# A second pair of sequences with two-level Strassen in the up-projections of a gated-scan and Hadamard-FFN kernel

## The chip, the cores and the metric

The kernel runs on one core of a Trainium2 chip, in float32 throughout. The metric is the device time of one execution in microseconds. The engines go by the names of the profile: PE (TensorE matmul), PEld (its weight loads), DVE (VectorE), ACT (ScalarE), POOL (GpSimd), SP (SyncE, which here only issues DMA transfers). Before the change the median of three runs is 791.53 us (791.39 to 792.0).

## The reference

```python
def attn(x, Wi, Wf, Wg, Wo, gnorm_w):            # x: (4, 512, 512)
    i, f, g = x @ Wi.T, x @ Wf.T, x @ Wg.T
    gate = sigmoid(f)
    v = silu(i) * (1 - gate)
    o = scan over t of  o[t] = gate[t] * o[t-1] + v[t]
    o = o * rsqrt(mean(o * o) + EPS) * gnorm_w * g * sigmoid(g)
    return o @ Wo.T

def ffn(x, W1, W2, W3):                          # hidden width 2048
    hidden = silu(x @ W1.T) * (x @ W3.T)
    return fwht(hidden) @ W2.T                   # Walsh-Hadamard along the 2048

x = x + layernorm(attn(layernorm(x), ...))
x = x + layernorm(ffn(layernorm(x), ...))
```

The batch is four sequences of 512 positions, each 512 wide. The transform is applied to W2 once instead of to the hidden values.

## The kernel before

**Strassen products.** Every large matrix product is cut into 2 x 2 blocks and made by seven block products in place of eight (the Winograd form; `ORDER` lists them, P1, P2, P6, P5, P7, P3, P4). The sums of blocks that this needs are made on DVE by `combine_left` (lines 156 to 163) and `combine_right` (165 to 173), each four adds or subtractions. The seven products of one unit go into three PSUM banks X, Y and Z; X is read out after P1, P6, P7 and P4, since each of them goes on from the sum before. A read-out (an "eviction") is a copy on ACT or an add on DVE (lines 492 and 494).

**Units.** An attention unit (`attn_unit`, three per sequence) and a single FFN unit (`ffn_unit`, for 2 x 128 of w1's and w3's columns, called a row block m; eight per sequence) are one such set of seven with 4 matmuls of 128 x 128 x 256 for each product, 28 in all (line 517). The products of the attention's output (`attn_out`, line 624) and of the FFN's output (`ffn_out`, line 684; four parts per sequence, 28 matmuls each) come piece by piece from the queue `fill` and stand between the products of a unit: one behind products 1, 3, 5 and 6, or behind all seven in a unit that is called dense.

**The pair.** For sequences 2 and 3 the FFN's up-projections are made together. The two sequences are the two column halves of one larger product, and a second Strassen level is laid over the first: `ffn_pair(g, down)` goes through seven outer steps (`OUTER`) of seven inner products ("leaves"), each 2 matmuls (line 879), 98 for two row blocks of both sequences. Each of the 49 leaves is evicted alone (ACT at line 889 for the plain products of outer P1 and P7, else DVE at line 892); some outer sums are added on POOL (894, 896). The weights of an outer step are loaded by `load_leaf_w` (four transfers of 128 KB, line 822) three steps ahead, and POOL makes their inner sums. `hidden` makes SiLU and the product (852, 860), and POOL combines half of the results. The down-projections of the group before (`down`, one matmul per piece) are spread between leaves 4 and 48.

The right-hand side of the pair, `xq`, lies in three double tiles and one single: B11 and B12 in `blocks[0]`, B21 and B22 in `blocks[1]`, T2 and T1 in `blocks[2]`, T4 alone. `transpose_pair` fills the first two from the folded copies of the normalized x; `combine_pair_early` makes T4 and T3 (four DVE operations of 128 x 1024), `combine_pair_late` makes T2 and T1 and the remaining inner sums, right before the pair.

**Folds.** A normalized x is written to DRAM by POOL (`xnd`, line 317), read back in 32-row blocks by SP (`load_fold`, eight transfers of 128 KB, line 437) and turned by 32 x 32 transposes on DVE (455, 770).

**The order.** After the attentions of sequences 0 to 2: FFN of sequence 0 (eight units), attention of sequence 3, FFN of sequence 1 (eight units), then the pair in four groups, then the last 56 down matmuls. In sequence 0's units w1 and w3 are read from the inputs, combined on DVE and kept in DRAM (`kept`, a POOL transfer); sequence 1 and the pair read them back. The steps for w2's transform (`low_pair`, `low_tile`, for four pairs of row blocks) stand beside units of sequence 0.

**Who sets the order.** PE's and SP's instructions run in the order of the code. For DVE, ACT and POOL a planner sets the order when the program is built, from estimated costs and from priorities (`high_priority`; evictions 400, steps beside them 200; `behind` and `issue_after` give an earliest place). At run time each engine's queue runs strictly in that order. Buffers are shared by tag: `w` (stream, 5), `w` (stream2, 4), `x` (3), `wide` (3), `xt` (2), `og` (1), `ht` (4); a tile waits until a buffer of its tag is free. `run` and `seven` hang the small steps (`acts`, `sums`, `scaled`, `beside`) behind products.

## Time and profile before

| | us |
|---|---|
| median of three runs | 791.53 |
| the profiled execution | 792.25 |
| its span, from the first to the last instruction | 790.5 |
| first instruction of the pair's products (line 879) | 490.0 |
| end of the last matmul | 780.45 |

The profile's parts used here: the busy time of each engine and its number of instructions; the span in 40 slices with the busy share in tenths; the chain of work that ended last, followed back from the end; groups of instructions by line with their mean duration; and, from the trace, the same by stretch (busy time of PE, its weight loads, DVE, ACT and POOL with the number of instructions, the granted clock, the DMA share and GB/s), the instructions in order of time, and the DMA transfers with the time from issue to landing. The granted clock is 0.996 over the span.

### The profile page before, as it was taken

To read this page: it belongs to the slowest core of one execution; us is meant where nothing else is said; L and a number is where in the kernel's file an instruction comes from. 1 tells how busy PE (TensorE), PEld (TensorE's weight loads), DVE (VectorE), ACT (ScalarE), POOL (GpSimd) and SP (SyncE) were. 2 spreads that over 40 slices of the span, in tenths; PEclk is the share of its full clock that TensorE was granted. 3 is DMA by queue.
4 is the path that set the end of the run, shared out by engine and by line. 5 is a ranking of instruction groups with operands and counts; after the bars stand their busy time and mean duration, and the time that the engine had idled before them with its cause. 6 is when DMAs were issued, how large, how long until landed. Compare 5 with 4: busy or idle time off the path is not lost.

```text
span 790.5 us, 10222 instructions
## 1 busy us (share of the span) xinstructions
PE 776.3 (98%) x3608; PEld 670.1 (85%) x3608; DVE 564.2 (71%) x1093; ACT 246.9 (31%) x348; POOL 245.5 (31%) x319
## 2 busy tenths in 40 slices
PE   9999999999999999999999999999999999999994
PEld 7888788888888888888888888888788888888884
DVE  6789889799789774477455459868755655765676
ACT  4374754543436212344223412011321200111112
POOL 2111202112213110001001005088947646672452
PEclk9999999999999999999999999999999999999998
DMA  9997445776997982538246736341521412141012
GB/s 296 398 340 299 156 198 180 218 258 244 339 336 289 340 325 102 160 150 347 94 187 200 267 78 221 131 122 33 195 80 54 157 53 58 49 166 54 1 53 108
DMA packets 78148, 144.93 MB, mean 183 GB/s; under 512 B 6160, under 2 KB 55952, under 8 KB 77712
## 3 DMA queue, kind: packets, MB, share of 16 engines
q1 hardware_dynamic: 68032, 96.82, 38.1%
q0 software_dynamic: 9344, 46.14, 14.9%
q10 hardware_dynamic: 720, 1.31, 0.4%
q8 instruction: 29, 0.48, 0.2%
q14 instruction: 23, 0.19, 0.1%
HBM read 97.06 MB, written 47.19 MB: 182 GB/s over the span
## 4 chain that ended last, share of the span: by engine, by line
PE 88%; DVE 5%; DMA 2%; POOL 1%; issue 1%; SPq 0%; ACT 0%; POOLq 0%; DVEq 0%
PE X_f L517 13%; PE X_po L684 13%; PE X_u L879 11%; PE X_a L517 10%; PE Z_po L684 7%; PE Z_f L517 6%; PE Z_u L879 5%; PE Z_a L517 5%; PE X_y L624 3%; PE Y_f L517 3%; PE Y_po L684 3%; PE Y_a L517 3%; PE Y_u L879 3%; PE Z_y L624 2%; DMA w2p<-in_W_dram 1%
## 5 line engine op out<-in xcount | busy, mean ns | idle before, releaser
L684 PE MATMUL X_po<-w,ht 128*128 128x256 f32 x512 | 132.1, 379 | 0.1
L517 PE MATMUL X_f<-xt_f,w 128*128 128x256 f32 x512 | 121.2, 380 | 0.1
L879 PE MATMUL X_u<-xq,wl 128*128 128x256 f32 x448 | 114.4, 381 | 2.3 <-ACT q L889 0.8
L517 PEld LDWEIGHTS X_f<-xt_f,w 128*128 128x128 f32 x512 | 96.8, 190 | 14.5 <-DVE d_f L492 0.5
L684 PEld LDWEIGHTS X_po<-w,ht 128*128 128x128 f32 x512 | 97.2, 190 | 13.7 <-DVE f L492 0.5
L879 PEld LDWEIGHTS X_u<-xq,wl 128*128 128x128 f32 x448 | 84.2, 190 | 17.1 <-issue 3.6
L892 DVE TENSOR_TENSOR q<-X_u,q 128x512 f32<-128x512 f32 x88 | 60.8, 691 | 42.6 <-PE X_u L879 41.7
L494 ACT COPY d_f<-X_f 128x512 f32<-128x512 f32 x48 | 28.0, 584 | 131.8 <-PE X_f L517 115.7
L684 PE MATMUL Z_po<-w,ht 128*128 128x256 f32 x256 | 66.4, 379 | 0.0
L492 DVE TENSOR_TENSOR f<-X_po,f 128x512 f32<-128x512 f32 x51 | 34.9, 685 | 36.9 <-PE X_po L684 36.9
L517 PE MATMUL Z_f<-xt_f,w 128*128 128x256 f32 x256 | 60.5, 379 | 0.0
L879 PE MATMUL Z_u<-xq,wl 128*128 128x256 f32 x224 | 57.6, 379 | 0.0
L684 PEld LDWEIGHTS Z_po<-w,ht 128*128 128x128 f32 x256 | 48.6, 190 | 6.8 <-DVE f L492 0.2
L517 PEld LDWEIGHTS Z_f<-xt_f,w 128*128 128x128 f32 x256 | 48.6, 190 | 6.6
L263 POOL TENSOR_TENSOR rs_f<-rs_f,power 128x2 f32<-128x2 f32 x16 | 13.4, 840 | 117.8 <-DVE nm_f L364 73.5
L852 ACT ACTIVATE q<-q 128x1024 f32<-128x1024 f32 x16 | 16.9, 1057 | 103.8 <-DVE q L892 58.2
L879 PEld LDWEIGHTS Z_u<-xq,wl 128*128 128x128 f32 x224 | 42.5, 190 | 6.0 <-DVE q L892 0.3
L892 DVE TENSOR_TENSOR q<-Z_u,q 128x512 f32<-128x512 f32 x48 | 33.1, 689 | 20.1 <-PE Z_u L879 19.5
L158 POOL TENSOR_TENSOR wl<-wl 128x256 f32<-128x256 f32 x28 | 21.3, 762 | 77.4 <-DMA wl<-s_w 70.2
L494 ACT COPY d_a<-X_a 128x512 f32<-128x512 f32 x36 | 21.1, 585 | 67.8 <-PE X_a L517 67.6
L889 ACT COPY q<-X_u 128x512 f32<-128x512 f32 x24 | 14.0, 584 | 89.4 <-PE X_u L879 76.8
L179 POOL DMA_DIRECT2D s_w<-w x24 | 13.1, 547 | 72.5 <-DVE w L163 56.9
(205 smaller groups left out, 1459.2 us busy)
## 6 DMA issues: line engine op xcount, KB each, us to landing
w<-s_w SPq DMA_DIRECT2D x32, 896.0 KB, 6.4
s_w<-w POOLq DMA_DIRECT2D x24, 896.0 KB, 6.9
wl<-s_w SPq DMA_DIRECT2D x112, 128.0 KB, 2.7
w<-in_W_dram SPq DMA_DIRECT2D x32, 256.0 KB, 6.4
wi<-s_wi SPq DMA_DIRECT2D x6, 896.0 KB, 9.3
wf<-s_wf SPq DMA_DIRECT2D x6, 896.0 KB, 5.4
wg<-s_wg SPq DMA_DIRECT2D x6, 896.0 KB, 6.3
w_h<-w2p POOLq DMA_DIRECT2D x8, 512.0 KB, 5.7
```

Of the source, the lines that this page charges most:

```text
L158: eng.tensor_add(t[:, S1], t[:, A21], t[:, A22])
L179: nc.gpsimd.dma_start(out=saved[key], in_=t)
L263: read["power"] = nc.gpsimd.tensor_tensor(r, r, power_t[:, 0:n], ALU.pow)
L492: read[what] = nc.vector.tensor_add(to, ps[which], to)
L494: read["copy"] = nc.scalar.copy(to, ps[which])
L517: nc.tensor.matmul(ps[:, n, :], w[:, a, c, :], xt[:, bb, c, :], start=first and n == 0 and c == 0, stop=c == 1, skip_group_check=True,)
L624: nc.tensor.matmul(ps[:, t, :], og[:, a, c, ts(t, P)], w[c][:, bb, :], start=first and t == 0 and c == 0, stop=c == 1, skip_group_check=True,)
L684: nc.tensor.matmul(ps[:, t, :], hts[b, m][:, a, ts(t, P)], w[m][:, W2[bb], :], start=first and k == 0, stop=m == ms[-1], skip_group_check= ...
L852: nc.scalar.activation(d[:, 0], d[:, 0], AF.Silu)
L879: nc.tensor.matmul(ps[which][:, k, :], w[:, k, a, :], x[:, bb, :], start=first and k == 0, stop=True, skip_group_check=True,)
L889: read["copy"] = nc.scalar.copy(y, ps[which])
L892: last = nc.vector.tensor_add(y, ps[which], z)
```

## The change

Only the first half of w1's and w3's row blocks (m = 0 to 3) is now made in single units for sequences 0 and 1. Their second half (m = 4 to 7) is made as a pair in two groups, before the four groups of sequences 2 and 3. The order becomes: four single units of sequence 0, attention of sequence 3, four single units of sequence 1 (the first two dense), two groups for the pair (0, 1), four groups for the pair (2, 3). Along with it:

- The weights of m = 4 to 7, which no single unit reads any more, are loaded one per single unit by `prepare_weight`, combined on POOL and kept.
- The folds of sequences 0 and 1 are held in buffers of tag `x` and turned beside units 1 and 2 of sequence 1; x of sequence 0 is kept in DRAM too, and read back before its last sum.
- The right-hand side of the second pair is made during the second group. Its folds are read in two halves (`load_half_fold`, 64 columns of every 128), at leaves 7 and 31; they are transposed at leaves 29, 31, 37 and 39; the early sums stand at leaves 43 to 49. The tiles `blocks[1]` and `blocks[2]` change places. 28 matmuls of the down-projection are kept back and run between the two pairs; POOL makes the inner sums of `blocks[0]` there.
- The down weights of a group are loaded within the group before their use (at leaf 7 or 14).
- The fourth sequence's attention uses other buffers (`x` for its normalized x and its fold, `xt` for its gated output), and its fold is loaded right before the unit in which it is transposed.

```diff
-            xns[name, b] = work.tile(
-                [P, NT, D], F32, tag="wide", name=f"xn_{name}_{b}", bufs=3
+            pool, tag = (xpool, "x") if (name, b) == ("a", 3) else (work, "wide")
+            xns[name, b] = pool.tile(
+                [P, NT, D], F32, tag=tag, name=f"xn_{name}_{b}", bufs=3
             )
...
-            both = work.tile([P, 2, G, P], F32, tag=tag, name=f"fold_{name}_{b}", bufs=3)
+            pool = xpool if tag == "x" else work
+            both = pool.tile([P, 2, G, P], F32, tag=tag, name=f"fold_{name}_{b}", bufs=3)
...
-            og = work.tile([P, 7, 2, H], F32, tag="og", name=f"og_{b}")
+            tag, bufs = ("xt", 2) if b == 3 else ("og", 1)
+            og = work.tile([P, 7, 2, H], F32, tag=tag, name=f"og_{b}", bufs=bufs)
...
-                        if b:
-                            keep_x(b, i)
+                        keep_x(b, i)
...
-    PAIR = 2, 3
+    PAIR = [0, 1]
+    GROUPS = 2, 3, 0, 1, 2, 3
...
-    def transpose_pair(j):
-
-        if not blocks:
-            blocks[0] = pair_tile("og", "xq_1")
-            blocks[1] = pair_tile("xt", "xq_2")
-            xq.update({B11: blocks[0][:, 0], B12: blocks[0][:, 1]})
-            xq.update({B21: blocks[1][:, 0], B22: blocks[1][:, 1]})
-        fold = folds.pop(("f", PAIR[j]))
-
-        def make(h):
-            for c in range(ND):
-                to = blocks[c // 2][:, j, INNER[c % 2, h]]
-                nc.vector.transpose(
-                    to.rearrange("p (g q) -> p g q", q=32), fold[h][:, :, ts(c, 32)]
-                )
-
-        return [partial(make, h) for h in range(2)]
+    def name_blocks(*which):
+        for k, pair in ((0, (B11, B12)), (1, (B21, B22)), (2, (T2, T1))):
+            if k in which:
+                xq.update({r: blocks[k][:, j] for j, r in enumerate(pair)})
+
+    def transpose_half(j, half, fold):
+
+        def make():
+            for h in range(2):
+                for c in range(2):
+                    to = blocks[half][:, j, INNER[c, h]]
+                    nc.vector.transpose(
+                        to.rearrange("p (g q) -> p g q", q=32), fold(h, 2 * half + c)
+                    )
+
+        return make
...
+    def inner(pair, steps=(0, 1), eng=None):
+        combine_right(pair.rearrange("p r s f -> p s r f"), eng or nc.vector, steps)
...
-        xq[T4] = work.tile([P, 7, H], F32, tag="o", name="xq_4")
+        if T4 not in xq:
+            xq[T4] = work.tile([P, 7, H], F32, tag="o", name="xq_4")
         t4 = raw(T4)
-        nc.vector.tensor_sub(t4, raw(B12), raw(B11))
-        nc.vector.tensor_sub(t4, raw(B22), t4)
-        nc.vector.tensor_sub(t4, raw(B21), t4)
-        nc.vector.tensor_sub(raw(B12), raw(B22), raw(B12))
+        return [
+            partial(nc.vector.tensor_sub, *args)
+            for args in (
+                (t4, raw(B12), raw(B11)), (t4, raw(B22), t4), (t4, raw(B21), t4),
+                (raw(B12), raw(B22), raw(B12)),
+            )
+        ]
...
+        if 2 not in blocks:
+            blocks[2] = work.tile([P, 2, 7, H], F32, tag="xt", name="xq_3", bufs=2)
+        name_blocks(2)
...
+    def load_half_fold(half):
+
+        G = T // 64
+        t = work.tile(
+            [P, 2, 2, G, P // 2], F32, tag="wide", name=f"fold_pair_{half}", bufs=3
+        )
+        half_folds[half] = t
+        for j, b in enumerate((2, 3)):
+            rows = xnd["f", b].rearrange("t p d -> (t p) d")
+            for h in range(2):
+                for i in range(4):
+                    cols = slice(i * P + half * P // 2, i * P + (half + 1) * P // 2)
+                    nc.sync.dma_start(
+                        out=t[ts(i, 32), j, h],
+                        in_=rows[ts(h, H), cols].rearrange("(g q) k -> q g k", q=32),
+                    )
+
+    def half_fold(j, half):
+        return lambda h, c: half_folds[half][:, j, h, :, ts(c % 2, 32)]
+
+    def whole_fold(b):
+        return lambda h, c: folds["f", b][h][:, :, ts(c, 32)]
...
-        g, k = divmod(n, len(OUTER))
-        if g == NU // NS:
+        at, k = divmod(n, len(OUTER))
+        if at == len(GROUPS):
             return
-        a = OUTER[k][1]
-        t = stream.tile([P, 2, 7, P], F32, tag="w", name=f"wl_{g}_{a}")
+        g, a = GROUPS[at], OUTER[k][1]
+        t = stream.tile([P, 2, 7, P], F32, tag="w", name=f"wl_{at}_{a}")
         for w, name in enumerate(("w1", "w3")):
             for i in range(NS):
                 nc.sync.dma_start(
...
+    def prepare_weight(src, name, m):
+        weight(src, name, m, 0)
+        key, t = uncombined.pop()
+        combine_left(t, nc.gpsimd)
+        kept(key, t)
+
+    def ffn_pair(at, down, events, hold=0):
+
+        g = GROUPS[at]
+        total, start = len(down) - hold, 3
...
+        tokens = dict(xq)
         for step, (outer, _, right, _, _) in enumerate(OUTER):
-            load_leaf_w(7 * g + step + AHEAD)
-            w, x = leaf_w.pop(7 * g + step), xq[right]
+            load_leaf_w(7 * at + step + AHEAD)
+            w, x = leaf_w.pop(7 * at + step), tokens[right]
...
+                for make in events.get(leaf, ()):
+                    with tc.issue_after(last.ins), tc.high_priority(offset=SOON):
+                        make()
...
-                load_ffn_w(b, m + 1)
-            if b == 0 and m == 5:
...
-                p, what, k = LOW[m]
...
-                fill.extend([None] * (4 if b else 2) + attn_out(2 + b))
-            if m and m % NS == 0:
-                fill.extend([None] + ffn_out(b, m // NS - 1))
-            if b and m % NS == 1:
...
-                load_x(3)
-            if b == 0 and m == 4:
-                late = dict(beside_copies(3, ((4, 3), (4, 5), (5, 0), (5, 3))))
...
-            if b == 0 and m == 6:
-                load_fold(3, "a")
-            if b == 0 and m == 7:
-                transpose_beside(3, "a")
-            if b == 1 and m in (4, 6):
-                load_fold(PAIR[m // 2 - 2], "f")
-            if b == 1 and m in (5, 6):
-                pair_beside(transpose_pair(m - 5), m - 5)
-            if b == 1 and m == 7:
-                pair_beside(
-                    [
-                        combine_pair_early,
-                        partial(inner, blocks[0]),
-                        partial(inner, blocks[1], (0,)),
-                    ]
-                )
-            if b == 1 and m == 7:
-                for k in range(AHEAD):
-                    load_leaf_w(k)
-            ffn_unit(b, m)
-            pace.update(FULL)
-            with behind("P7"), tc.high_priority(offset=SOON):
-                combine_weights()
-        if b == 0:
-            load_attn_w(3, 0)
...
-                else:
-                    load_ffn_w(1, 0)
-                    transpose_beside(1, "f")
-                if u == 1:
-                    load_fold(1, "f", "ht")
-                attn_unit(3, u)
...
+    LATER = [(name, m) for m in range(NS * 2, NU) for name in ("w1", "w3")]
+    SOURCE = {"w1": w1, "w3": w3}
+
+    def solo_unit(b, m, dense=False):
+        if m + 1 < 2 * NS:
+            load_ffn_w(b, m + 1)
+        name, later_m = LATER.pop(0)
+        prepare_weight(SOURCE[name], name, later_m)
+        ffn_unit(b, m, dense)
+        pace.update(FULL)
+        with behind("P7"), tc.high_priority(offset=SOON):
+            combine_weights()
...
+    load_x(3)
+    fill.extend([None] * 2 + attn_out(2))
+    solo_unit(0, 0)
+    spread_low(0, "combined", 0)
+    late = dict(beside_copies(3, ((1, 3), (1, 5), (2, 0), (2, 3))))
+
+    def beside_unit(m):
+        for (unit, k), step in late.items():
+            if unit == m:
+                beside.setdefault(k, []).append(step)
+
+    beside_unit(1)
+    solo_unit(0, 1)
+    fill.extend([None] + ffn_out(0, 0))
+    beside_unit(2)
+    solo_unit(0, 2)
+    load_low(1)
+    load_fold(3, "a", "x")
+    spread_low(1, "P2", 2)
+    transpose_beside(3, "a", ((3, "P2"), (4, "P7"), (6, "P3")))
+    load_attn_w(3, 0)
+    solo_unit(0, 3)
...
+    load_low(2)
+    fill.extend([None] + ffn_out(0, 1))
+    load_attn_w(3, 1)
+    attn_unit(3, 0)
+    load_attn_w(3, 2)
+    spread_low(2, "P2", 0)
+    load_fold(1, "f")
+    attn_unit(3, 1)
+    load_ffn_w(1, 0)
+    transpose_beside(1, "f")
+    attn_unit(3, 2)
+
+
+    places = (1, "P2"), (4, "P7"), (6, "P3")
+    fill.extend([None] * 4 + attn_out(3))
+    for b in PAIR:
+        load_fold(b, "f", "x")
+    solo_unit(1, 0, True)
+    blocks[0] = work.tile([P, 2, 7, H], F32, tag="og", name="xq_1")
+    pair_beside([transpose_half(j, 0, whole_fold(j)) for j in range(2)], places)
+    solo_unit(1, 1, True)
+    load_down_w(1, 0)
+    blocks[1] = ogs[3].rearrange("p a c f -> p (a c f)").rearrange(
+        "p (r s f) -> p r s f", r=2, s=7
+    )
+    name_blocks(0, 1)
+    early = combine_pair_early()
+    pair_beside(
+        [transpose_half(j, 1, whole_fold(j)) for j in range(2)]
+        + [lambda: [make() for make in early]],
+        places,
+    )
+    solo_unit(1, 2)
+    fill.extend([None] + ffn_out(1, 0))
+    load_low(3)
+    spread_low(3, "P2", 2)
+    pair_beside([partial(inner, blocks[0]), partial(inner, blocks[1], (0,))], places)
+    for k in range(AHEAD):
+        load_leaf_w(k)
+    solo_unit(1, 3)
+    for b in PAIR:
+        folds.pop(("f", b))
...
     with tc.high_priority(offset=SOON):
         combine_pair_late()
-    reload_x(1, work, "wide")
-    down = [make for make in fill if make] + ffn_out(1, NU // NS - 1, True)
+    load_down_w(1, 1)
+    down = [make for make in fill if make] + ffn_out(1, 1, True)
...
-    for g in range(NU // NS):
-        load_down_pair(g)
-        ffn_pair(g, deque(down))
-        down = [
-            part
-            for b in PAIR
-            for part in ffn_out(b, g, True)
-        ]
+    ffn_pair(0, deque(down), {14: [partial(load_down_pair, 2)]})
+    down = deque(part for b in PAIR for part in ffn_out(b, 2, True))
+
+
+    early = []
+
+    def early_step(k):
+        if not early:
+            early.extend(combine_pair_early())
+        early[k]()
+
+    def exchange():
+        blocks[1], blocks[2] = blocks[2], blocks[1]
+        name_blocks(0, 1)
+
+    ffn_pair(
+        1,
+        down,
+        {
+            7: [partial(load_half_fold, 0)],
+            14: [partial(load_down_pair, 3)],
+            29: [transpose_half(0, 0, half_fold(0, 0))],
+            31: [transpose_half(1, 0, half_fold(1, 0)), partial(load_half_fold, 1)],
+            37: [exchange, transpose_half(0, 1, half_fold(0, 1))],
+            39: [transpose_half(1, 1, half_fold(1, 1))],
+            43: [partial(early_step, 0)],
+            45: [partial(early_step, 1)],
+            47: [partial(early_step, 2)],
+            49: [partial(early_step, 3)],
+        },
+        28,
+    )
+    with tc.high_priority(offset=SOON):
+        inner(blocks[0], eng=nc.gpsimd)
+        inner(blocks[1], (0,))
+    while down:
+        down.popleft()()
+    with tc.high_priority(offset=SOON):
+        combine_pair_late()
+    down = [part for b in PAIR for part in ffn_out(b, 3, True)]
+    reload_x(0, work, "wide")
+
+
+    PAIR[:] = 2, 3
+    for at in range(2, len(GROUPS)):
+        g = GROUPS[at]
+        events = {7: [partial(load_down_pair, g)]}
+        if g == 0:
+            events[42] = [partial(reload_x, 1, work, "wide")]
+        ffn_pair(at, deque(down), events)
+        down = [part for b in PAIR for part in ffn_out(b, g, True)]
     for b in PAIR:
         reload_x(b, xpool, "x")
     for part in down:
```

## The prediction

> **What bounds the kernel now.** I read the page from the top: busy time, slices, chain; then TensorE's chain in order of time, to price one matmul; then busy time by stretch, to see where TensorE loses time.
>
> ```profile
> PE 776.3 (98%) x3608; PEld 670.1 (85%) x3608; DVE 564.2 (71%) x1093; ACT 246.9 (31%) x348; POOL 245.5 (31%) x319
> PE   9999999999999999999999999999999999999994
> DVE  6789889799789774477455459868755655765676
> POOL 2111202112213110001001005088947646672452
> PE 88%; DVE 5%; DMA 2%; POOL 1%; issue 1%; SPq 0%; ACT 0%; POOLq 0%; DVEq 0%
> ```
>
> PE is busy in every slice and carries 88% of the chain: this program takes as long as its matmuls. DVE is high in the first half; POOL works only behind slice 24, where the pair begins. So two prices matter: a matmul, and a stretch in which another engine makes PE wait.
>
> ```profile
> 766.64 3.45 PE X_po L684 x16
> ```
>
> The page lists each f32 matmul as two instructions (512 for line 684's X bank, where the code has 256). So 3.45 us hold 8 matmuls: **0.4315 us** each. Now the stretches (columns: PE, its weight loads, DVE, ACT, POOL busy with instructions; clock; DMA):
>
> ```profile
> 300.00:340.00 40.00, 40.00 (x187) 35.22 (x186) 18.46 (x28) 11.47 (x15) 0.00 (x0) 1.00 0.47 149
> 490.00:518.00 28.00, 27.20 (x122) 22.22 (x120) 25.68 (x39) 3.78 (x6) 9.16 (x10) 1.00 0.39 132
> 518.00:540.00 22.00, 22.00 (x103) 19.38 (x102) 12.51 (x20) 2.34 (x4) 19.83 (x25) 1.00 0.26 74
> 540.00:572.00 32.00, 31.22 (x141) 26.13 (x140) 26.91 (x50) 8.25 (x12) 28.37 (x37) 1.00 0.40 131
> 572.00:640.00 68.00, 67.22 (x312) 58.88 (x311) 38.24 (x58) 12.79 (x19) 45.50 (x58) 1.00 0.28 90
> 640.00:740.00 100.00, 100.00 (x464) 87.77 (x463) 61.26 (x93) 12.27 (x18) 54.87 (x64) 1.00 0.23 72
> ```
>
> A full stretch holds one instruction per 0.2157 us and some 1.6 for the edges (300 to 340: 185.4 + 1.6 = 187, as shown). By that, 490 to 518 lacks 9.4 instructions, **2.0 us**; 540 to 572 lacks 8.9, **1.9 us**; 572 to 640 lacks 4.8, 1.0 us; the others 0.3 in all. The first is the passage from single units into the pair (the last right-hand sums, DVE busy 92%); the second holds the norm and residual of one finished sequence (DVE 84%). A check: the pair part has 392 + 224 + 28 + 16 matmuls, 284.8 us, and lasts from 490.2 to 780.45, 290.2 us: 5.4 lost, against 5.2. So PE waits little, and only where DVE comes near 90%.
>
> **The matmuls.** A single unit has 28 matmuls, a pair group 98 for what four single units do with 112. Two sequences' second half is eight units, 224, and becomes two groups, 196. 28 x 0.4315 = **-12.1 us**, all on the path. Nothing else of PE's changes in number; attention and the down-projections only move.
>
> **Eight weights combined on POOL.** POOL gets 8 x 4 subtractions of 128x512 (1.27 us by line 894), 40.6 us over eight single units of 12 to 24 us (28 matmuls and 0 to 28 of the fill), where it was busy 10 to 20%; DVE loses 8 x 4 of 0.69, 22 us. PE lost at most 0.13 us in the single units (352 to 490: 137.87 of 138), so the relief can gain nothing. What it can cost is two engines in one another's way:
>
> ```profile
> 491.96 1.74 DVE L795 TENSOR_TENSOR xq<-xq,xq 128x1024 f32<-128x1024 f32 x1
> 492.58 1.70 POOL L162 TENSOR_TENSOR wl<-wl 128x256 f32<-128x256 f32 x1
> 495.36 1.21 DVE L796 TENSOR_TENSOR xq<-xq,xq 128x1024 f32<-128x1024 f32 x1
> 517.80 0.72 POOL L158 TENSOR_TENSOR wl<-wl 128x256 f32<-128x256 f32 x1
> ```
>
> Beside POOL the DVE operation takes 0.53 us longer; POOL's goes from 0.72 to 1.70. Nothing, if evictions (one input from PSUM, 0.69 throughout) keep their time; at most one eviction late by 0.42 per weight (0.68 became 1.10 at line 169), 3.4 us. The nearer row is the single units' idle DVE, so I take **+0.7**. [...]
>
> **The fourth sequence's fold** now loads one unit before its use, not two: eight transfers, 0.45 us each to issue and 4.9 to land (10.4 at most), 8.5 to 14.0 us. The transposes stand behind the unit's fourth product and two of the fill, 10.4 us in. 0 to +3.6; I take **0**, the median. SP's queue is ordered by hand: what stands behind the fold are the attention's weights, a unit early. Also at nothing: the fourth attention (same products, same fill), the stores of sequence 0's x (POOL issues, 0.56 us each), and the gate tile in the other buffer, whose product now comes 8.6 us behind the unit (five products) rather than 15.5, with muls of 1.21 and sums of 0.69 in front; without that cover, 1 us.
>
> **The passage into the first pair** has the same sums as today, 2.0 us, already counted, but shorter units ahead of them. Unit 2 of sequence 1 now has no fill (12.1 us) and unit 3 three products (17.3): 29.4 us for DVE's own share of two units 8.6, 8 transposes 2.8, four subtractions of 1024 4.5, seven inner sums 4.2, the last low-frequency step of w2 (4 of 512 and two tiles of 1.96) 6.3 and some 5 of the fourth norm, 31.4 us (prices per start, see below). 2 us more than fit go on into the pair: nothing if DVE catches up in the group (518 to 540: 57% busy), 2.0 again if it costs as much as the first surplus; I take the middle, **+1.0**. POOL has one weight more (5.1 us) in front of a leaf's 2.9, and the down weights for the next group leave SP's queue there, which was behind the 0.6 us that PE's load waited for POOL at 517. -0.6 to +5.1; the leaf is needed some 20 us in, so 0 for POOL.
>
> **The passage from pair to pair** is new. Group 1 (98 + 28 matmuls, 54.4 us) takes in 16 transposes and four 128x1024 subtractions, and 28 down matmuls are kept back behind it, 12.1 us. From leaf 42 to leaf 14 of the next group PE has 6.0 + 1.7 + 12.1 + 12.1 + 5.9 = 37.8 us. DVE, by starts in a row in the timeline (0.60 us for 512 columns, 1.13 for 1024, 0.355 for a transpose, 0.34 for 256): 36 evictions and gate products 21.6, 8 transposes 2.8, six of 1024 6.8, 8 inner sums 4.8, T4's four 1.4: 37.4 us. DVE is as full as PE. Nothing if the 12.1 us cover it; the nearest row, 490 to 518 at 92%, lost 2.0. With POOL's four inner sums beside it I take **+2.5**. Upper end: the half folds.
>
> ```profile
> fold_f<-xnd_f SPq DMA_DIRECT2D x32, 128.0 KB, 5.6
> L437 SPq DMA_DIRECT2D fold_f<-xnd_f x32: 302/450/1039, 134.9 to 456.8; - x32
> ```
>
> One is 16 transfers: 16 x 0.45 + 5.6 = 12.8 us, in runs of 256 bytes where today's are 512. Upper bound: a whole fold of the same 1 MB took some 10.5 us (issued 452.0 to 456.8, 5.7 to land), double packets 21. The second can start only when the first's transposes free its buffer, about 36 us into group 1; its transposes stand at leaf 37, 41.0 us in. DVE runs in order: a transpose that waits holds every eviction behind it, and PE stops when the banks are full. Today no transpose waits for a fold, and DVE's order is planned from costs, not by the leaf alone. Above, 57 - 41 - 1.3 (PE's run-on) = +14.7. [...]
>
> **Two finished sequences in one group.** The third group now holds both norms and residuals, where 540 to 572 paid 1.9 us for one: 0 to +3.8, I take **+1.9**. Two more group boundaries (572 to 640: 1.0 us; later 0.2): **+1.0**. The tail behind the last matmul, 780.45 to 790.5, is untouched.
>
> **The sum.** -12.1 + 0.7 + 1.0 + 2.5 + 1.9 + 1.0 = -5.0. The profiled execution took 792.25 us (790.5 its span), 0.72 above the median of 791.53. 792.25 - 5.0 = 787.2; as a median **786.5 us**, a ratio of 0.994.
>
> **Rivals.**
> (A) *All of it is hidden.* For: single units lose nothing, a middle group 0.2 us. Only matmuls count: 791.5 - 12.1 = 779.4.
> (B) *DVE becomes the bound from group 1's last third to the fourth group.* For: 37.4 beside 37.8 us; the third group adds two norms to 60%. Against: the first passage at 92% cost only 2.0. If each of the two stretches is paid double and the POOL term is 3.4: 786.5 + 2.5 + 1.9 + 2.7 = 793.6 at its worst, its middle 790.
> (C) *The second half fold arrives late and DVE stands behind it: slower than before.* One mechanism, at the transposes of leaf 37. For: 41.0 comes before 36 + 12.8. Against: no transpose waits today. Price 14.7 in place of 2.5: 798.7. The gain without that term is 7.5 us; PE runs on for 1.3, so it is gone when DVE waits 8.8 us, until 49.8, which is a half fold of about 14 us.
> (D) *The matmuls don't go away:* the count in the code excludes it.
>
> **Chances.** Forecast (783 to 788) 0.50, A 0.16, B 0.20, C 0.14. The range runs from A to the far end of B and leaves out most of C: 779.4 to 793.6. A measurement of this kernel tells about 0.2%, 1.6 us, from no change. Faster: 0.50 + 0.16 + 0.10 of B + 0.02 of C (a short block) = 0.78. Within 0.2%: 0.07 of B, 0.03 of C, 0.10. Slower: 0.03 of B, 0.09 of C, 0.12.
>
> **What the new profile should show.** PE instructions 3608 - 56 = 3552, PE busy about 766 us. POOL busy to about 380 us. Single units still with PE at full count. The passage from pair to pair with DVE above 90% and some 2 to 3 us lost; if transposes stand with a DMA as releaser there, C is at work. The third group with DVE near 85% and twice the loss of 540 to 572. I am wrong if PE loses time in the single units, or if a wait for a leaf's POOL sums shows at each group's start.

## The result, and the profile after

The changed kernel takes **838.64 us** (median of 4 runs, 836.81 to 840.9) where the kernel before takes 791.76 (4 runs, 791.39 to 792.22): a ratio of 1.0593 (95% interval 1.0558 to 1.0628), slower by 46.9 us. The four runs lie in two pairs, 836.8 and 840.4 to 840.9, so a difference of less than some 4 us between the medians of a few runs shows nothing by itself. The prediction said 786.5, within 779.4 to 793.6. The profiled execution has a span of 835.0 us (before 790.5) and a mean granted clock of 0.969 (before 0.996).

The page of the kernel after: busy time, three engines and the clock in 40 slices of 20.9 us, and the chain by engine:

```profile
PE 778.6 (93%) x3552; PEld 666.8 (80%) x3552; DVE 617.8 (74%) x1129; ACT 237.2 (28%) x332; POOL 374.2 (45%) x461
PE   9999999996959999988999995899799999999995
DVE  6789798878865675899576689878555655665676
POOL 2111113223512012292698439747765754781462
PEclk9999999997979999999999997999899999999998
PE 55%; DVE 9%; POOL 5%; DMA 3%; issue 3%; SPq 0%; ACT 0%; POOLq 0%; DVEq 0%
```

The 56 instructions went as counted. But PE, at nine tenths or more in all slices but the last before, now has holes, in the single units too (slices 10 and 12), and PE's share of the chain fell from 88% to 55%. To size the holes I took the start of each matmul from the trace and added up what the distance to the next exceeds 0.2157 us by. That sum was 9.5 us before and is 66.4 after. The difference of 56.9, less 12.1 for the matmuls, gives 44.8; the span grew by 44.5. Five places, 58.0 us together, hold the whole result; the rest of the program loses 8.4:

| place | us lost | where |
|---|---|---|
| A, 187 to 199 | 10.5 | second single unit of sequence 0 |
| B, 237 to 250 | 11.3 | start of the fourth attention |
| C, 363 to 401 | 9.2 | passage from single units to the first pair |
| D, 506 to 530 | 15.8 | passage from pair to pair |
| E, 573 to 605 | 11.2 | group with the two finished sequences |

By stretch (PE, its loads, DVE, ACT, POOL busy with instructions; clock; DMA), the places are, in order, A, B, two parts of C, D, two parts of E:

```profile
187.00:199.00 12.00, 3.78 (x9) 3.06 (x10) 8.79 (x23) 0.75 (x2) 4.60 (x7) 0.58 0.41 149
237.00:251.00 14.00, 5.38 (x14) 3.79 (x14) 8.36 (x18) 1.21 (x3) 1.27 (x2) 0.63 1.06 331
363.00:379.00 16.00, 13.21 (x59) 10.80 (x59) 16.00 (x23) 6.80 (x9) 11.88 (x12) 1.00 0.38 139
384.00:394.00 10.00, 7.29 (x25) 5.03 (x24) 9.99 (x22) 3.85 (x5) 2.60 (x3) 0.83 0.84 285
506.00:531.00 25.00, 13.60 (x43) 10.68 (x43) 24.86 (x25) 2.35 (x4) 21.26 (x16) 0.73 0.47 177
573.00:576.00 3.00, 0.98 (x5) 0.59 (x4) 2.72 (x3) 0.00 (x0) 2.92 (x3) 1.00 0.00 0
593.00:606.00 13.00, 6.84 (x20) 5.22 (x19) 8.28 (x17) 2.63 (x4) 8.88 (x13) 0.74 0.28 106
```

In A, B and E, DVE is not full: it waits. In D, and in C in this execution, it is. In all but the first part of C and the short part of E the clock is down as well.

**A.** POOL in order of time (start, duration, line, the wait before it in brackets):

```profile
184.59 0.72 POOL L158 TENSOR_TENSOR w<-w 128x256 f32<-128x256 f32 x1 [8.56 <-DMA w<-in_W_dram]
...
187.78 0.57 POOL L179 DMA_DIRECT2D s_w<-w  x1 [0.30 <-POOL w L163]
188.38 1.38 POOL L263 TENSOR_TENSOR rs_a<-rs_a,power 128x2 f32<-128x2 f32 x2
```

Line 263 is the last step of a norm's inverse root, the power of -0.5, on two columns. In POOL's order it stands behind the sums of a later weight, and those wait 8.56 us for the weight to land. DVE and PE in the same stretch:

```profile
189.13 0.16 DVE L294 SCALAR_TENSOR_TENSOR nb_a<-mv_a,rs_a 128x2 f32<-128x2 f32 x1 [5.67 <-POOL rs_a L263]
...
194.48 0.68 DVE L494 TENSOR_TENSOR d_f<-X_f,d_f 128x512 f32<-128x512 f32 x1
```

```profile
195.22 3.78 PE L519 MATMUL X_f<-xt_f,w 128*128 128x256 f32 x8 [8.41 <-DVE d_f L494]
```

DVE waits 5.67 us for that power, and the eviction that PE needs stands behind it, with 5.4 us of other DVE work between. After 8.41 us of idling PE's next 8 instructions take 3.78 us; at 0.2157 they take 1.73.

**B.** SP's waits between 195 and 240 us, and DVE at the end of them:

```profile
SPq L439 <- DMA xnd_a<-xn_a: 16.6, 1, 16.6
```

```profile
239.69 1.42 DVE L457 STREAM_TRANSPOSE xt_a<-fold_a 128x256 f32<-128x256 f32 x4 [3.69 <-DMA fold_a<-xnd_a]
```

The fold's first transfer is issued at 230.51, because the normalized x of the fourth attention is written only at 221.8 to 226.8 (four ACT operations of line 309): its buffer, now of tag `x`, is free only after the kept x of sequence 1 has been stored (issued at 199.39, landed at 208.21), and in ACT's planned order the four stand together behind that. The fold is not alone: the attention's first weight stands behind it on SP's queue, is issued at 236.95 and lands 8.6 us later, at 245.5, where PE goes on (245.66). So PE waits for the fold and for the weight about equally long.

**D.** DVE has short waits for PE ahead of the last transposes (first fence), then the sums; POOL's inner sums follow in the second fence:

```profile
499.98 0.69 DVE L494 TENSOR_TENSOR f<-Z_po,f 128x512 f32<-128x512 f32 x1 [1.04 <-PE Z_po L686]
501.70 0.69 DVE L494 TENSOR_TENSOR f<-X_po,f 128x512 f32<-128x512 f32 x1 [1.03 <-PE X_po L686]
503.43 0.69 DVE L494 TENSOR_TENSOR f<-Z_po,f 128x512 f32<-128x512 f32 x1 [1.03 <-PE Z_po L686]
504.04 0.76 DVE L767 STREAM_TRANSPOSE xq<-fold_pair 128x256 f32<-128x256 f32 x2
...
507.98 2.87 DVE L1357 TENSOR_TENSOR xq<-xq,xq 128x1024 f32<-128x1024 f32 x2
510.77 1.21 DVE L169 TENSOR_TENSOR xq<-xq 128x512 f32<-128x512 f32 x1
511.90 2.28 DVE L797 TENSOR_TENSOR og<-xq,xq 128x1024 f32<-128x1024 f32 x1
```

```profile
496.23 1.04 POOL L158 TENSOR_TENSOR ht<-ht 128x256 f32<-128x256 f32 x1 [12.84 <-DVE ht L893]
...
509.73 1.70 POOL L163 TENSOR_TENSOR wl<-wl 128x256 f32<-128x256 f32 x1
511.40 1.71 POOL L168 TENSOR_TENSOR xq<-xq 128x512 f32<-128x512 f32 x1
513.18 2.12 POOL L169 TENSOR_TENSOR xq<-xq 128x512 f32<-128x512 f32 x1
```

```profile
515.36 2.08 PE L913 MATMUL X_u<-xq,wl 128*128 128x256 f32 x4 [8.51 <-POOL xq L169]
```

The third product of the new group needs an inner sum of the first double tile. Two queues lead to it. On DVE: last transposes at 504.04, early sums to 510.85. On POOL: from 496.23 on, without a break, eight sums of hidden values and eight of weights, to 511.43, and the inner sums behind them. PE's kept-back matmuls end at 505. The half folds are not in it (transfers, KB each, median us to landing):

```profile
fold_f<-xnd_f SPq DMA_DIRECT2D x32, 128.0 KB, 4.9
...
fold_pair<-xnd_f SPq DMA_DIRECT2D x32, 64.0 KB, 2.1
```

No transpose of a half fold waits for a transfer.

**E.** POOL, then DVE:

```profile
594.31 0.73 POOL L163 TENSOR_TENSOR wl<-wl 128x256 f32<-128x256 f32 x1
594.99 0.72 POOL L263 TENSOR_TENSOR rs_f<-rs_f,power 128x2 f32<-128x2 f32 x1
```

```profile
595.75 0.75 DVE L369 SCALAR_TENSOR_TENSOR xr<-f,rs_f,xr 128x512 f32<-128x512 f32 x1 [6.96 <-POOL rs_f L263]
```

The power stands behind 16 sums in a row (583.22 to 595.04); DVE waits 6.96 us at it, PE idles 6.2.

### The profile page after: what moved, and what is told of

It reads as the page before. It is cut to its first block, busy times and chain, and to the rows that moved or that the text cites. A ratio compares the mean times of both kernels' runs of the same rounds, so it can differ in the third digit from the quotient of the medians.

```text
span 835.0 us, 10444 instructions
## 1 busy us (share of the span) xinstructions
PE 778.6 (93%) x3552; PEld 666.8 (80%) x3552; DVE 617.8 (74%) x1129; ACT 237.2 (28%) x332; POOL 374.2 (45%) x461
## 3 DMA queue, kind: packets, MB, share of 16 engines
q0 software_dynamic: 9632, 47.19, 14.5%
## 4 chain that ended last, share of the span: by engine, by line
PE 55%; DVE 9%; POOL 5%; DMA 3%; issue 3%; SPq 0%; ACT 0%; POOLq 0%; DVEq 0%
PE X_u L913 14%; PE X_po L686 10%; PE Z_u L913 7%; PE Z_po L686 5%; PE X_f L519 4%; PE Y_u L913 3%; PE Y_po L686 3%; PE X_a L519 3%; PE Z_f L519 2%; PE X_y L627 1%; PE Z_a L519 1%; DMA wf<-s_wf 1%; DMA wl<-s_w 1%; POOL q L928 1%; PE Y_f L519 1%
## 5 line engine op out<-in xcount | busy, mean ns | idle before, releaser
L926 DVE TENSOR_TENSOR q<-X_u,q 128x512 f32<-128x512 f32 x132 | 90.9, 688 | 57.5 <-PE X_u L913 56.5
L519 PE MATMUL X_f<-xt_f,w 128*128 128x256 f32 x256 | 62.5, 389 | 10.1 <-DVE d_f L494 10.1
L926 DVE TENSOR_TENSOR q<-Z_u,q 128x512 f32<-128x512 f32 x72 | 49.5, 688 | 26.4 <-PE Z_u L913 25.5
L519 PEld LDWEIGHTS X_f<-xt_f,w 128*128 128x128 f32 x256 | 49.1, 194 | 18.6 <-DVE d_f L494 11.1
L913 PE MATMUL X_u<-og,wl 128*128 128x256 f32 x192 | 50.4, 386 | 1.3 <-DVE q L926 0.6
L928 POOL TENSOR_TENSOR q<-q,q 128x512 f32<-128x512 f32 x24 | 30.4, 1273 | 37.3 <-DVE q L926 37.2
L926 DVE TENSOR_TENSOR q<-Y_u,q 128x512 f32<-128x512 f32 x42 | 28.9, 687 | 22.3 <-PE Y_u L913 22.3
L893 DVE TENSOR_TENSOR ht<-q 128x512 f32<-128x512 f32 x48 | 36.7, 781 | 8.3 <-PE X_po L686 7.0
L913 PEld LDWEIGHTS X_u<-og,wl 128*128 128x128 f32 x192 | 36.4, 192 | 7.8 <-issue 1.5
L519 PE MATMUL X_a<-xt_a,wi 128*128 128x256 f32 x128 | 34.2, 390 | 8.6 <-DVE xt_a L457 8.5
```

Source lines behind the costliest of these rows:

```text
L519: nc.tensor.matmul(ps[:, n, :], w[:, a, c, :], xt[:, bb, c, :], start=first and n == 0 and c == 0, stop=c == 1, skip_group_check=True,)
L893: nc.vector.tensor_mul(t[:, h : h + 3 : 2], d[:, 0, n].rearrange("p (t f) -> p t f", t=2), d[:, 1, n].rearrange("p (t f) -> p t f", t=2),)
L913: nc.tensor.matmul(ps[which][:, k, :], w[:, k, a, :], x[:, bb, :], start=first and k == 0, stop=True, skip_group_check=True,)
L926: last = nc.vector.tensor_add(y, ps[which], z)
L928: nc.gpsimd.tensor_add(part(0, i, j), part(0, i, j), part(3, i, j))
```

## The experiments

All edits are to the changed kernel except where the kernel before is named; two or more runs each. Times are medians beside 838.64, losses are counted as above.

**The power left out.**

```diff
-        read["power"] = nc.gpsimd.tensor_tensor(r, r, power_t[:, 0:n], ALU.pow)
+        read["power"] = read["rs"]
```

> The changed kernel, with the inverse root of every norm left out (the power on POOL is gone, the scale is the variance plus epsilon): so no norm waits for POOL's queue. Theory Q (POOL's strict queue: the power of a norm stands behind weight sums, the next step on DVE waits for it, and every eviction behind that waits too): the two stalls that stand behind a power, 186 to 195 us and 588 to 600 us, go, about 9 and 8 us, and some 2 us at 572; 838.6 becomes 815 to 822. [...]

> The kernel before, with the inverse root of every norm left out in the same way. It shows what the omission itself is worth where POOL has little to do. Theory Q: 0 to 2 us (one residual at 566 waited 0.9 us for its power), 789.5 to 791.5. [...] If it gains 5 us or more, the difference of the other kernel is no sign of the queue.

Measured: 823.16 us after (ratio 1.0398, 1.0368 to 1.0428), 790.47 before (0.9984, 0.9972 to 0.9995). So the same two columns cost 15.5 us in the one kernel and 1.3 in the other. A falls to 4.4, E to 0.5; B rises to 15.3, since PE there waits 12.5 us for the attention's first weight, so the 15.5 are what is left over. What stays of A is not a wait of DVE, which has no pause there; PE waits 2.7 us for the same eviction. The stretch of E:

```profile
570.00:606.00 36.00, 35.88 (x166) 30.89 (x165) 31.84 (x55) 9.98 (x14) 30.61 (x38) 1.00 0.51 174
```

PE is full beside a DVE at 88% and a POOL at 85%: in E it was the order, not the volume.

**The later weights summed on DVE** (the single units' own sums take them on). Rival D, in this run and in a_inner, has DVE's volume as the bound.

```diff
     def prepare_weight(src, name, m):
         weight(src, name, m, 0)
-        key, t = uncombined.pop()
-        combine_left(t, nc.gpsimd)
-        kept(key, t)
```

> The changed kernel, with the eight later weights combined on DVE behind the unit, as the others are, instead of on POOL. Theory Q: the stall at 186 to 195 goes (9 us) and the waits for POOL around 365 to 385 shrink; DVE takes 22 us more in units that have room; 825 to 832. Rival D: DVE gets 22 us more, and the kernel gets slower: 840 or more.

Measured: 833.25. A falls from 10.5 to 2.0, with DVE at 97% there:

```profile
184.00:204.00 20.00, 19.32 (x97) 16.53 (x96) 19.42 (x53) 7.01 (x10) 6.55 (x9) 1.00 0.82 301
```

C is 14.7 here, but it reaches 14.5 in a_inner too, which has the orders of the changed kernel up to there; so it is not shown that the weights on DVE cost anything at C.

**Three tries to get the power past the sums on POOL**: the power with the evictions' priority (a_urg), the sums placed behind the unit's P7 (a_late), the sums one unit after the load (a_ahead).

```diff
-        read["power"] = nc.gpsimd.tensor_tensor(r, r, power_t[:, 0:n], ALU.pow)
+        with tc.high_priority(offset=URGENT):
+            read["power"] = nc.gpsimd.tensor_tensor(r, r, power_t[:, 0:n], ALU.pow)
...
         ffn_unit(b, m, dense)
+        with behind("P7"):
+            combine_left(t, nc.gpsimd)
+            kept(key, t)
...
+        loaded.append(uncombined.pop())
+        if len(loaded) > 1:
+            sum_weight()
```

> The changed kernel, with one thing more: the planner places the power of each norm on POOL at the evictions' priority, ahead of weight sums that are ready at the same time. The result is the reference's. Theory Q: the stall behind the residuals of sequences 0 and 1 (573 to 605 us, 11.2 us lost) goes, as it did when the power was left out; the one at 187 stays for the most part, since there POOL waits for a transfer that the planner took for landed: 826 to 830. Rival (the power's own time on POOL, or DVE's work, is the cost): no change, 836 to 840.

> The changed kernel, with POOL's sums of a later weight placed behind the seventh-but-two product of the unit instead of at its head, so that the weight's transfer has landed when POOL comes to it. Theory Q: the loss at 187 to 199 us (10.5) falls to 1 to 4 us as with the sums on DVE, and DVE has no more to do: 829 to 834. [...]

> Each of the eight later weights is loaded one single unit before POOL sums it, so that POOL finds it landed. Theory W (POOL stands 8.6 us at a weight's transfer, and the norm's power stands behind it on POOL's queue): that wait goes, the loss at 187 to 199 us falls from 10.5 to 1 to 4 us, the time to 829 to 834. Rival V (what holds the power back is the sums' own time beside a busy DVE): the loss stays above 8 us and the time at 837 to 842.

Measured: 841.66, 840.84, 839.96; A 11.1 in each. None moved what it meant to move: in all three traces POOL still stands 8.6 us at a weight's transfer and the power comes after the sums, and at E it still stands behind 16 sums (DVE waits 6.9 us). Why the planner keeps this order is not shown; presumably it takes the weight for landed, or the power's input for late. Since the order is the same at both places, these runs say nothing for or against the theory.

**The root on ACT and DVE** (whole computation).

```diff
-        read["power"] = nc.gpsimd.tensor_tensor(r, r, power_t[:, 0:n], ALU.pow)
+        nc.scalar.activation(r, r, AF.Sqrt)
+        read["power"] = nc.vector.reciprocal(r, r)
```

> The inverse root of every norm is made off POOL, as a square root on ACT and a reciprocal on DVE; the computation is whole. Theory P (DVE waits for the power, which stands behind POOL's bulk sums): the losses at 187 to 199 and 573 to 605 us, 10.5 and 11.2 us, fall to 1 to 5 and 0 to 2, the time to 822 to 829, as with the power left out (823.2). Rival T (ACT now changes its function table between a square root and the others 37 times more, and its evictions wait for that): the gain is eaten, 833 to 845, and new waits of PE or DVE for ACT show.

Measured: 836.9. E falls to 1.7 and A to 5.7, as theory P has it, but ACT now loads a table 17 times for the roots, 1283 ns each, and 21 times for the other functions; the losses before 110 us grow by 6.4 and at B by 3.2, with 4.9 us of PE waiting for ACT's copies. Each theory is right in part, and the two nearly cancel:

```profile
L263 ACT ACT_TABLE_LOAD x17 | 21.8, 1283 | 0.3
```

**The fourth normalized x in another buffer** (tag `xt` in place of `x`).

```diff
-            pool, tag = (xpool, "x") if (name, b) == ("a", 3) else (work, "wide")
+            tag, bufs = ("xt", 2) if (name, b) == ("a", 3) else ("wide", 3)
```

> The changed kernel, with the fourth sequence's normalized x in a buffer of tag xt, which is free there, instead of a buffer of tag x, which is free only when x of sequence 1 has been kept. Theory S (the fold is late because its source waits for that buffer): the four normalizations move ahead by 10 us or more, and the loss at 237 to 250 us (11.3) falls below 3: 826 to 831. Rival (the fold is late because the stall at 187 pushes everything, or because SP's queue is full): it stays at 8 to 12: 835 to 840.

Measured: 829.64 (1.0479, 1.0435 to 1.0522), 9.0 us less; B falls from 11.3 to 0.6. The first of the four operations now starts at 190.58, the last ends at 215.61, and the fold is issued at 223.07. The buffer was the cause.

**C: w2's last low-frequency step two units earlier.**

```diff
+    load_low(3)
+    spread_low(3, "P2", 2)
     solo_unit(1, 0, True)
```

> The changed kernel, with the last step of w2's transform beside the first single unit of sequence 1 (dense, with room on DVE) instead of the last, so that DVE has 6.3 us less just ahead of the first pair. Theory D (DVE has a backlog at that passage): the loss from 363 to 401 us (9.2) falls to 2 to 5; 831 to 835. Theory Q alone (POOL's weight sums block there): no change at that place, 836 to 840.

Measured: 845.05. C is 11.6, not 2 to 5, and 4.1 us are lost at the new place. The theory that C would go with this step falls.

**D: the first double tile's inner sums on DVE (a_inner), all 56 down matmuls kept back (a_hold), the steps at leaves ahead of the evictions (a_soon), the four inner sums left out (a_noin).**

```diff
-        inner(blocks[0], eng=nc.gpsimd)
+        inner(blocks[0])
...
-        28,
+        56,
...
-                    with tc.issue_after(last.ins), tc.high_priority(offset=SOON):
+                    with tc.issue_after(last.ins), tc.high_priority(offset=URGENT + SOON):
...
-        inner(blocks[0], eng=nc.gpsimd)
         inner(blocks[1], (0,))
```

> The changed kernel, with the four inner sums of the first double tile at the passage from pair to pair on DVE instead of POOL. Theory Q: the first products there waited 8.5 us for POOL, whose four sums took 1.7 to 2.2 us each and stood behind eight weight sums; on DVE they are 4 x 0.6 us early in the passage; 5 to 9 us go: 830 to 834. Rival D: DVE is the limit there and gets 2.4 us more; 838 to 842.

> All 56 down matmuls of the second group are kept back for the passage from pair to pair, not 28 of them: 12.1 us more of PE's work there, and 12.1 us less in the group before. Theory Q (the sums of the second pair's right-hand side take more DVE and POOL time than PE has work for): the loss at 506 to 530 us falls from 15.8 to 4 to 9 us, the time to 828 to 835. Rival O (DVE's planned order puts the transposes and first sums behind evictions that come only as PE goes on, so that more work of PE delays them as well): the loss stays at 13 to 18 us, the time at 836 to 843; then DVE has idle stretches of about 1 us between evictions ahead of the last transposes, more of them than now.

> The steps of the second pair's right-hand side that stand at leaves of a group (transposes, early sums) go ahead of the evictions in priority; PE's and SP's orders are the same. Theory O (the planned order leaves DVE idle for 3 us at 498 to 504 us and starts the sums late): the sums start earlier, the loss at 506 to 530 us falls from 15.8 to 9 to 13 us, the time to 832 to 836. Rival Q (the volume of the sums): DVE's work stays the same and the loss at 14 to 18 us, the time at 837 to 841.

> The four inner sums of the first double tile of the second pair are left out (the output is then wrong for two sequences). Theory Q (the passage from pair to pair is short of DVE and POOL time, POOL's four sums of 1.7 to 2.2 us and DVE's 128x1024 of 2.3 us slowing one another): PE's wait of 8.5 us for a POOL sum goes and the DVE operations are nearer 1.2 us, the loss at 506 to 530 us falls from 15.8 to 4 to 9 us, the time to 827 to 833. Rival D (DVE's own chain of sums holds PE by itself): the loss stays at 11 to 16 us, the time at 834 to 840.

Measured: 839.39, 845.14, 836.2, 828.82; D 14.6, 13.7, 9.5 and 1.4 (a_hold loses 9.5 more in the group before, a_soon 1.7). In a_inner the inner sums on DVE come just as late: transposes at 509.53, early sums to 516.34, inner sums to 520.33, and PE waits 8.1 us for them; moving them off one of the two queues gains nothing. In a_hold 12 us more of cover do not help, and PE waits even longer at the same product:

```profile
529.62 2.08 PE L913 MATMUL X_u<-xq,wl 128*128 128x256 f32 x4 [9.97 <-POOL xq L169]
```

There DVE's early sums are done at 516.46, but POOL begins its 16 other sums only at 508.07, after gate products of DVE that stand behind evictions, and evictions come only as PE goes on:

```profile
508.07 0.73 POOL L158 TENSOR_TENSOR ht<-ht 128x256 f32<-128x256 f32 x1 [18.19 <-DVE ht L893]
...
526.96 1.26 POOL L168 TENSOR_TENSOR xq<-xq 128x512 f32<-128x512 f32 x1
```

With the steps ahead of the evictions (a_soon; PE's order is the same) 6 us of D go and PE waits for evictions instead, 3.7 and 3.1 us. Without the last link D is gone:

```profile
508.00:533.00 25.00, 24.74 (x112) 20.64 (x111) 24.35 (x34) 3.40 (x5) 21.02 (x21) 1.00 0.56 200
```

DVE is at 97% and POOL at 84% here, as full as in D, and PE loses nothing to speak of. So D is the order on two queues more than a volume: in the loss at D, rival O is right against Q for a_hold and theory O against rival Q for a_soon. The run a_noin alone does not separate the two: it takes away POOL's four sums (7.8 us) with the link, and it made the planner put evictions between DVE's other sums, so the 13 us are not the link's alone.

**Several at once.** a_xpn takes the other buffer, no power and no inner sums together; a_xpnw also the weights on DVE. a_xss is the other buffer, the root on ACT, and the steps ahead; a_xws the other buffer, the weights on DVE, and the steps ahead; a_xwsl that, with

```diff
+    load_attn_w(3, 0)
     load_fold(3, "a", "x")
     spread_low(1, "P2", 2)
     transpose_beside(3, "a", ((3, "P2"), (4, "P7"), (6, "P3")))
-    load_attn_w(3, 0)
```

> Three causes at once: the fourth sequence's normalized x in the other buffer (as in the run with that alone), the power left out of every norm, and the four inner sums of the second pair's first double tile left out; the output is wrong. If the three places are separate and no more stands behind them, the gains add: 9.0 + 15.5 + 9.8 = 34.3 us below 838.6, 801 to 808. Rival: behind each stall the next one comes up (POOL's and DVE's volume is the bound), and the time stays above 812.

> The same three, and the eight later weights summed on DVE (as in the run with that alone, 5.4 us, which came from the place at 187 to 199 us where the power has already taken 6.1 of 10.5). If the first passage is bound by DVE's volume, the four sums more there cost what the place gains: 799 to 808. If POOL's sums of these weights still hold PE somewhere, 794 to 799.

> A whole computation with three repairs: normalized x in the other buffer, the inverse root on ACT and DVE, and the steps at leaves ahead of the evictions. By the gains of each (9.0, some 12, 2.4): 812 to 819. Rival T (ACT's tables): 822 to 836.

> A whole computation with three repairs that each gained alone: normalized x in the other buffer (9.0), later weights summed on DVE (5.4), steps at leaves ahead of the evictions (2.4). If the places are separate: 818 to 825. Rival: as in the run with three causes taken away, the fourth attention comes up again (there its weights, which stand behind the fold on SP's queue, were waited for 4.6 and 2.2 us) and the time is 825 to 832.

> The same, with the fourth attention's first weights issued ahead of its fold on SP's queue. If the weights behind the fold are what is left at 225 to 250 us, the waits for a weight go and the time is 2 to 8 us below the run without this; if the fold and its transposes are as late as the weights, within 2 us of it, and PE's wait there is for the transposes.

Measured: 805.09, 802.74, 829.73, 824.62 (one run 820.37, one 828.88) and 825.89. In a_xpn the sum comes out (34.3 expected, 33.6 found), but not place by place: B is 14.0, hardly less than the 15.3 with the power left out alone, while D falls by 14.3 where 9.8 were counted. So that the places are separate is not shown. What is left there, over the 6.6 us at the program's start that the kernel before has too, is 14.0 at the fourth attention, 9.3 at C and 2.8 at A. The fourth attention came up again with another releaser:

```profile
PE X_a L519 <- DMA wi<-s_wi: 4.6, 1, 4.6
PE X_a L519 <- DMA wf<-s_wf: 2.2, 1, 2.2
```

(us, times, the longest). On SP's queue the attention's weights stand behind the fold: in a_ahead and a_hold, too, PE waits at B for them, 8.7 and 8.5 us. But with the weights in front (a_xwsl) the time stays within 1.3 us, and the wait is for the transposes:

```profile
PE X_a L519 <- DVE xt_a L169: 6.2, 1, 6.2
```

So the fold's whole chain (norm, store, load, transposes) is late there, and its weights just beside it. The three whole computations gain 8.9, 14.0 and 12.8 us; none comes near the kernel before, which is still 4% faster than the best of them.

**C stays open.** Its size differs from one execution to the next: 9.2 us in the profiled run of the changed kernel, 12.5 in a_soon, some 13 in a_noin and 14.5 in a_inner, all with the same orders up to there (with a hole of 2 us at 430 to 437 where there is one). With the power left out it is 9.4, with the low-frequency step elsewhere 11.6, with the weights on DVE 14.7 (16.0 in a_xpnw); so none of these differences is clear of that spread. Nor is it the volume on DVE alone. DVE is busy 16.00 of 16 us in the one profile, but in a_soon PE loses more beside a DVE at 12.76:

```profile
363.00:379.00 16.00, 12.02 (x49) 9.85 (x48) 12.76 (x18) 6.28 (x8) 15.03 (x16) 0.89 0.24 83
372.81 0.68 DVE L294 SCALAR_TENSOR_TENSOR nb_f<-mv_f,rs_f 128x2 f32<-128x2 f32 x1 [3.24 <-POOL rs_f L263]
375.40 2.05 PE L913 MATMUL X_u<-xq,wl 128*128 128x256 f32 x4 [3.98 <-POOL w L159]
```

DVE waits for a norm's power here too. (The sum that the last row names as PE's releaser ended at 374.41, so what released PE is not clear.) And in the second part of C, PE waits for a down weight's transfer, in the changed kernel (first row; it is issued only at 384.48) and in a_soon (second row):

```profile
PE X_po L686 <- DMA w<-s_w: 1.8, 1, 1.8
PE X_po L686 <- DMA w<-s_w: 4.3, 2, 2.7
```

With the low-frequency step elsewhere that transfer is issued at 373.92 and PE does not wait for it. How the loss divides among DVE's volume, the power and the transfer was not tried apart.

## Why the prediction was wrong, point by point

The matmuls went as forecast, and the rest did not: five terms that the sum put at 6.1 us together came to some 54 (58.0, less the 3.9 that the two passages of the kernel before had lost already). Each was priced by the volume of work, and what the runs show in four of the five is an order: what stands in front on a strict queue, or what frees a buffer.

- **The matmuls, -12.1 us: right in number.** 3552 instructions, as said. The prediction's "PE busy about 766 us" (3552 x 0.2157 = 766.2) was 778.6: behind the long holes, where the granted clock is 0.50 (195 to 198, 246 to 250, 515 to 519, 600 to 605 us), PE's instructions take 0.42 to 0.55 us each from start to start in place of 0.2157, and those 12.4 us are part of the losses above. No term of the sum had it.
- **Eight weights combined on POOL, +0.7 (0 to 3.4): the step that failed.** It priced POOL's sums by what they do to DVE operations that run at the same time. It did not ask what stands behind them on POOL's own queue. The power of each norm does (line 263), DVE waits for it in order, and evictions wait behind DVE: A, 10.5 us. Taken off POOL, the weights give back 5.4 us net, and A falls to 2.0. The sums themselves were taken too large: the prediction has 32 of 128x512 at 1.27 us, 40.6 in all; the traces have 128x256, 28.1 us in all after the change, and 0.42 each on DVE before. So the term failed although the volume was smaller than thought. The prediction named its own test ("I am wrong if PE loses time in the single units"), and that is what the profile shows.
- **Two finished sequences, +1.9 (0 to 3.8): 11.2.** It was taken as DVE's volume, "DVE near 85% and twice the loss". DVE's volume costs nothing there (PE 35.88 of 36 us with the power left out). The cause is the same as in A: the power behind 16 sums.
- **The fourth sequence's fold, 0 (0 to 3.6): 11.3.** The cover of 10.4 us was compared with the time from the fold's first issue to its landing. But the issue itself was late: the diff's first lines put the normalized x into a buffer of tag `x`, and what frees that buffer was not followed. With another buffer the loss is 0.6. The attention's weights behind the fold, put at nothing because they are issued "a unit early", landed as late as the fold was turned.
- **The passage into the first pair, +1.0 over 2.0: 9.2, up to 14.5 in other executions.** That 2 us of DVE's work over would cost 2 at most was wrong. The sum also had no term for the down weight's transfer (1.8 to 4.3 us of waiting) and none for the power there (3.24 in a_soon). How much each of them costs stays open.
- **The passage from pair to pair, +2.5: 15.8.** Volumes were compared, 37.4 us of DVE beside 37.8 of PE. That they fit says nothing about order: transposes, early sums, inner sums, third product, with evictions in between on DVE and 16 other sums in front on POOL. DVE and POOL nearly as busy cost 1.4 us when the last link is missing.
- **Two more group boundaries, +1.0: about right.** Between 406 and 500 us and behind 605 the groups lose 2.8 us; the middle groups before lost 1.2.
- **The half folds, up to +14.7: not late.** The bounds were 12.8 and about 21 us; the first took 8.0 us to issue and 2.1 to land. No transpose waited for one: rival C ended on the right side of zero for a reason that did not occur.
- **Rivals A and B** are out by the result; D by the count.
- **Two engines in one another's way** was sized by two rows, 0.53 us longer for DVE (1.74 against 1.21) and 0.98 for POOL (1.70 against 0.72). At D POOL's 128x512 takes 1.71 to 2.24 us (1.27 in the mean of line 928) and DVE's 128x1024 up to 2.28 (1.21 in the mean of line 1328), while evictions keep 0.69. 1.21 and 1.27 are 2.48, so the longest come near to the two times one after the other, and the prediction's rows were milder; what holds the two engines up is not shown.

## What to carry to other kernels

When work goes to a less busy engine, list the small operations that stand behind it on that engine's queue and who waits for them: here two columns of a norm, held up by bulk sums, cost 15.5 us where they had cost 1.3. An edit may move a loss instead of removing it: with the power gone, B rose by 4.0. When a tile changes its tag, follow what frees the new buffer; and when work is squeezed into a passage, draw the chain that ends at the next product, on every queue that leads to it, not only the sum of busy time. Before a small gain is read from one place, see how much that place differs between runs with the same orders: here by 5 us at C. Behind the holes of 6.2 to 8.5 us at A, B, D and E the granted clock was 0.50 here, and PE's next 8 to 12 instructions took 1.8 to 2.7 us more than at 0.2157 each.

## What was not expected of the hardware

- The clock. At A PE stops at 186.80; the granted clock by stretch:

```profile
188.00:190.00 2.00, 0.00 (x0) 0.00 (x0) 0.38 (x3) 0.00 (x0) 1.73 (x3) 0.76 0.55 229
190.00:192.00 2.00, 0.00 (x0) 0.00 (x0) 2.00 (x5) 0.00 (x0) 0.00 (x0) 0.50 0.57 229
...
198.00:200.00 2.00, 2.00 (x8) 1.65 (x7) 2.00 (x4) 0.93 (x2) 1.07 (x2) 0.68 1.06 340
200.00:204.00 4.00, 4.00 (x21) 3.51 (x20) 3.26 (x10) 2.02 (x3) 0.30 (x1) 1.00 1.01 275
```

  By the means of the first and third row (an estimate, with 1.00 and 0.50 on the two sides of each step) it falls to half at about 189.0, 2.2 us after PE stopped, and is back at about 199.3, 4.1 us after PE resumes at 195.22. At C it fell behind a pause of 1.84 us (0.60 from 390 to 392, 0.54 from 392 to 394), and behind one of 2.02 at 573 to 576 it stayed at 1.00; what decides is not shown here.
- Transfers of 64 KB in runs of 256 bytes landed in 2.1 us, those of 128 KB in runs of 512 in 4.9 (medians of 32 each, at different places of the program).
- One ACT table load took 1.28 us (a_sqrt, the mean of 17 at line 263).
